# Buffers, preparation order and a state copy on GpSimd in a four-layer scan and window-attention kernel

## The chip, the cores and the metric

One core of one Trainium2 chip runs the whole program. The metric is device time in microseconds of one execution; the median of three executions is compared. Engines are named as in the profile: PE (TensorE matmul), PEld (its weight loads), DVE (VectorE), ACT (ScalarE), POOL (GpSimd) and SP (SyncE, which here only issues DMAs).

## The reference

The input x is (8, 56, 56, 192) in float32: eight images of 3136 pixels. Layer 0 splits the channels in two: the left 96 go through two 3x3 convolutions and a 1x1 one, the right 96 through a layer norm, a projection, a depthwise 3x3 convolution and a four-direction selective scan gated with a silu. Layers 1 and 2 are such scans alone, and layer 3 is a shifted-window attention (7x7 windows, six heads) with an MLP. The heart of layers 0 to 2 is the scan, over all 3136 pixels, in four orders k, for 192 channels d with 16 states n each:

```python
def step(h_prev, t):
    x_t, dt_t, B_t, C_t = t
    dA = jnp.exp(dt_t[..., None] * A)
    dBx = (dt_t * x_t)[..., None] * B_t[:, :, None, :]
    h = dA * h_prev + dBx
    y = jnp.einsum('bkdn,bkn->bkd', h, C_t)
    return (h, y)
```

Here dt is softplus of a small projection of x ("delta" below), and B and C are rows of another projection ("bc" below). Layer 3 in short:

```python
xw = jnp.roll(x, (-SS, -SS), axis=(1, 2))          # cut into 7x7 windows
attn = softmax(cos_sim(q, k) * scale + bias + mask)
x1 = shortcut + _ln(roll_back(attn @ v @ proj), norm1)
out = x1 + _ln(gelu(x1 @ fc1) @ fc2, norm2)
```

## The kernel before

**Scan steps.** `run` (L795) walks through 9216 steps: 8 images x 3 layers x 4 directions x 4 chunks of 784 pixels (a `Unit`) x 24 steps. A step has 128 partitions, 32 channels times 4 states, and 784 pixels. The 24 steps of a unit are two halves h of 12; a half is 96 channels, in 4 groups of states sg and 3 groups of channels j. One step s does, spread over five turns of the loop:

- `make` (L1037): ACT's exp of dsp (delta spread over the states) into a PSUM tile ps_x, of which there are two, and POOL's product db = usp x bt (du spread, and a B row broadcast), into one of four buffers;
- one turn later DVE's scan over ps_x and db. For three steps of four it writes ps_x, and DVE's product with ct gives hc. For each fourth (t % 4 == 3) the scan writes hc itself, and one turn later POOL multiplies hc by ct in place ("its own products");
- two turns after `make`, ACT copies the last column of the scan into `state` (L855), from which the same channels start in the next chunk, except after a last chunk;
- four turns later PE adds three hc into ps_y (`add_up`), and ACT merges ps_y into the layer's output.

Within a turn the order of issue is: state copy of s-2, exp and db of s, scan and product of s-1, POOL's product of s-2, `add_up`, `merge`, and then the pieces of other work. Every engine carries out its instructions in the order in which they are issued.

**Other work.** It is written as generators in three queues, and a yield of n puts the rest n turns off. `ahead` holds `prepare`, which makes delta and du for a half and spreads them with DMAs: two softplus pieces of 392 columns (matmul into a PSUM bank ps_p, relu into `delta`, abs, exp, ln and so on into `spe`, and POOL's add into `delta`), POOL's product `du`, then for each j the DMAs of `dsp` and `usp`, each with four buffers. `delta` and `du` have one buffer. `urgent` holds what follows a finished layer (`after`, and `project`, which writes the bc rows through the tile `bcx` to DRAM). `back` holds the next image's `ssm_front` and `conv_front` and the previous image's `attention_block`. At each turn pieces of `ahead` are issued freely, and those of the other two while a budget of charged PE and ACT time is left; SPARE and MOST (L1385) are its income and ceiling. `need` issues pieces at once, whatever turn it is, when a result is missing. All matmuls of other work share two PSUM banks; `all_banks` hands them out, the higher rank first.

**L3's rows.** `rows` (L1098) treats a row of eight windows: it loads a bias, the MLP's weights, runs `attention` and `mlp`, and `store` (L1354) transposes the result in four pieces, copies each to `ot` and stores it with DMAs on SP. The tag "wide" of pool q1 is one buffer that `qn`, `asq` and `hid` use in turn; `ot` shares the tag "pt" (two buffers of pool q2). After the last scan step, the last image's attention runs four rows at a time with six more banks (ps_t).

Of the kernel before, what the change touches and what calls it, by code (L numbers as in the profile page):

```python
# [31 lines left out]
F32 = mybir.dt.float32  # L32
# [4 lines left out]
HW = 56  # L37
L = HW * HW
C = 192
CH = 96  # L40
T = 448
ROWS = T // HW
NR = L // T
# [3 lines left out]
CK = 784  # L47
# [91 lines left out]
class Net:  # L139
    def __init__(self, ctx, tc, a, out):  # L140
        self.tc, self.nc, self.a, self.out = tc, tc.nc, a, out
        self.cp = ctx.enter_context(tc.tile_pool(name="const", bufs=1))
        self.dram = ctx.enter_context(tc.tile_pool(name="dram", bufs=1, space=bass.MemoryType.DRAM))
        self.dram2 = ctx.enter_context(
            tc.tile_pool(name="dram2", bufs=2, space=bass.MemoryType.DRAM)
        )
        ps = ctx.enter_context(tc.tile_pool(name="psp", bufs=1, space=bass.MemoryType.PSUM))
        self.banks = deque(ps.tile([128, 512], F32, name=f"ps_p{n}") for n in range(2))
        self.constants(ctx)
        self.wout = self.const("wout", [CH, 2, C])  # L150

        self.scans = ctx = ctx.enter_context(ExitStack())
        self.psum = ctx.enter_context(tc.tile_pool(name="psum", bufs=2, space=bass.MemoryType.PSUM))
        self.psum1 = ctx.enter_context(tc.tile_pool(name="psum1", bufs=1, space=bass.MemoryType.PSUM))
        big = ctx.enter_context(tc.tile_pool(name="big", bufs=1))
        self.bufs = [big.tile([CH, 2, L], F32, name=f"act{n}") for n in range(2)]
        for n in (1, 2, 3, 4, 5):
            setattr(self, f"s{n}", ctx.enter_context(tc.tile_pool(name=f"s{n}", bufs=n)))
        self.s6 = ctx.enter_context(tc.tile_pool(name="s6", bufs=HCS))
        self.ranks = self.s1.tile([CH, CK], F32, name="dts")  # L160
        self.aux = [self.s1.tile([CH, 2, HC], F32, name=f"aux{n}") for n in range(2)]
        self.nc.gpsimd.memset(self.ranks, 1.0)
        self.biasd = self.dram.tile([WT, 4, HEADS, WT], F32, name="biasd")
        self.done = set()
        self.nc = Engines(tc.nc)
        self.load = self.nc.load
        self.now, self.rank, self.asked = 0, 0, [-9] * 3
        self.ahead, self.urgent, self.back = deque(), deque(), deque()
        self.u0, self.sz, self.xl, self.u3, self.bcd = {}, {}, {}, {}, {}

# [195 lines left out]
            yield 2  # L366


    def bank(self, spare=0):


        (p,) = yield from self.all_banks(1, spare)
        return p

    def all_banks(self, n, spare=0):
        rank = self.rank
        while len(self.banks) < n + spare or any(at >= self.now - 1 for at in self.asked[rank + 1 :]):
            self.asked[rank] = self.now
            yield 1
        self.asked[rank] = -9  # L380
        return [self.banks.popleft() for _ in range(n)]
# [109 lines left out]
    def ssm_front(self, b):  # L491
# [3 lines left out]
        with tc.tile_pool(name="f1", bufs=1) as f1, tc.tile_pool(name="f2", bufs=2) as f2:  # L495
# [12 lines left out]
            grid = lambda p: p.rearrange("p (a b) -> p a b", a=ROWS)  # L508

            def depthwise(r, c, u):  # L510
                held = yield from self.bank(1)
                p = held[:CH, :T]
                for tap in range(9):
                    dy, dx = tap // 3, tap % 3
                    nc.tensor.matmul(
                        p, diag[:, c, tap, :], pads[r % 3][:, c, dy : dy + ROWS, dx : dx + HW],
                        start=tap == 0, stop=tap == 8,
                    )
                    if tap % 3 == 2:
                        yield 1  # L520
                yield 1
                nc.scalar.activation(u[:, c, :], p, AF.Identity, bias=self.v("conv2d_b", c))
                self.free(held)
                yield 1

            def gate(xnt, r, e, sz):
# [11 lines left out]
                self.free(held)  # L538
                yield 1

            for r in range(NR + 1):
                sz = u = None
                if r < NR:
                    tok = self.tokens(f2, b, r, "tokr", CH, C)
                    mv = f2.tile([TP, 4, 2], F32, name="mv")
                    rs = f2.tile([TP, 4], F32, name="rs0")
                    yield 2
                    for i in range(4):
                        st = f2.tile([TP, 6], F32, name="bnst")
                        nc.vector.bn_stats(st, tok[:, i, :])  # L550
                        nc.vector.bn_aggr(mv[:, i, :], st)
                        yield i % 2
                    nc.scalar.activation(rs, mv[:, :, 1], AF.Ln, bias=self.eps[:TP])
                    nc.scalar.activation(rs, rs, AF.Exp, scale=-0.5)
                    yield 1
                    for i in range(4):
                        nc.vector.tensor_scalar(
                            tok[:, i, :], tok[:, i, :], mv[:, i, 0:1], rs[:, i : i + 1],
                            ALU.subtract, ALU.mult,
                        )  # L560
                    yield 1
                    held = yield from self.bank()
                    p = held[:CH, :T]
                    for i in range(4):
                        nc.tensor.transpose(
                            p[:, i * TP : (i + 1) * TP], tok[:, i, :], self.ident[:TP, :TP]
                        )
                    yield LAG
                    xnt = f1.tile([CH, T], F32, name="xnt")
                    self.affine(xnt, p, self.v("ln_g"), self.v("ln_b"))  # L570
                    self.free(held)
                    yield 1
                    self.bottom(pads, r)
                    sz = f2.tile([CH, 2, T], F32, name="sz")
                    yield from self.together(2, [gate(xnt, r, e, sz) for e in range(4)])
# [13 lines left out]
    def conv_front(self, b):  # L589
# [3 lines left out]
        with tc.tile_pool(name="f1", bufs=1) as f1, tc.tile_pool(name="f2", bufs=2) as f2:  # L593
# [4 lines left out]
            grid = lambda p: p.rearrange("p (a b) -> p a b", a=ROWS)  # L598

            def conv(w, pads, r):  # L600
                held = yield from self.bank(1)
                p = held[:CH, :T]
                for tap in range(9):
                    dy, dx = tap // 3, tap % 3
# [7 lines left out]
                return p, held  # L612

            def first(r):
                tok = self.tokens(f2, b, r, "tokl", 0, CH)
                yield 2
                held = yield from self.bank()
                p = held[:CH, :T]
                for i in range(4):
# [21 lines left out]
            def third(r):  # L641
# [30 lines left out]
                yield from self.together(2, [last(c) for c in range(2)])  # L672
                nc.sync.dma_start(out=xld[:, :, r * T : (r + 1) * T], in_=xl)

            yield 2
            for r in range(NR + 2):
                if r < NR:
# [70 lines left out]
    def project(self, g, par, i):  # L748
# [7 lines left out]
        for q in range(2 * i, 2 * i + 2):  # L756
# [5 lines left out]
                    start=c == 0, stop=c == 1,  # L762
                )
            yield LAG
            t = self.s1.tile([128, HC], F32, name="bcx")[:W]
            nc.scalar.copy(t, p)
            self.free(held)
            yield 1
# [8 lines left out]
    def piece(self, queue, force=False):  # L777

        if not queue or (queue[0].at > self.now and not force) or queue[0].work.gi_running:
            return False  # L780
        task, rank = queue[0], self.rank
        self.rank = 2 if queue is self.ahead else int(queue is self.urgent)
        if not task.go(self.now):
            queue.remove(task)
        self.rank = rank
        return True
# [8 lines left out]
    def run(self):  # L795
# [25 lines left out]
        self.step = 0  # L821
        self.ahead.append(Task(self.prepare(units[0], 0, 0)))
        self.need(("half", 0))
        self.ahead.append(Task(self.prepare(units[0], 1, half)))
        for sg in range(NSG):
            self.load_bc(units[0], sg)
        made, weighed, copies = {}, {}, deque()
# [1 line left out]
        for s in range(S + 8):  # L829
            self.now += 1  # L830
            self.step = s
            for e in left:
                left[e] = min(left[e] + SPARE[e], MOST[e])

            t = s + half + 1
            if t < S and t % half == 0:
                self.ahead.append(Task(self.prepare(*steps[t][:2], t)))
            if s < S and s % half == 0:
                self.need(("half", s))
                U = steps[s][0]  # L840
                if s % (16 * NG) == 0:
                    if U.l == 0:
# [9 lines left out]
            if 0 <= t < S and not steps[t][0].last:  # L852
                U, h, sg, j = steps[t]
                end = CK - 1 if U.k < 2 else 0
                nc.scalar.copy(self.at_state(h, sg, j), made[t][:, end : end + 1])  # L855
            made.pop(t, None)
            if s < S:
                made[s] = self.make(*steps[s])
# [178 lines left out]
    def make(self, U, h, sg, j):  # L1037
# [3 lines left out]
        x = self.ps("x", 128, CK)  # L1041
        col = U.k * NG + (h * 3 + j) * NSG + sg
        self.nc.scalar.activation(x, d, AF.Exp, scale=self.A[U.l][:, col : col + 1])
        db = self.s4.tile([128, CK], F32, name="db")
        self.nc.gpsimd.tensor_mul(db, ub, self.B_[U, sg])
        return x, db

# [50 lines left out]
    def rows(self, b, wis, wqkv, wpr, f1b, q1, q2):  # L1098
# [18 lines left out]
        for n, wi in enumerate(wis):  # L1117
# [1 line left out]
            bias = q1.tile([WT, 2, HEADS, WT], F32, name="biasl")  # L1119
            kind = 2 * (wi == NW - 1)  # L1120
            nc.sync.dma_start(out=bias, in_=self.biasd[:, kind : kind + 2])
            yield 2
            wf1 = []
            for half in range(2):
                wf1.append(q2.tile([CH, 2, FF // 2], F32, name="wf1", tag="wf"))
# [3 lines left out]
            o = yield from self.mlp(x, f1b, wf1, q1, q2)  # L1129
            if n + 1 < len(wis):  # L1130
                x = yield from load(wis[n + 1])
            yield from self.store(o, wi, b, q2)

    def attention(self, x, wi, bias, wqkv, wpr, q1, q2):

# [215 lines left out]
        yield from self.block_norm(o, "n2", x, o, sq)  # L1351
        return o

    def store(self, o, wi, b, q2):  # L1354
        nc = self.nc

        def store(a):
            n = min(2, WS - a) * HW
# [4 lines left out]
                    p[:, CH * c : CH * c + CH], o[:, c, a * HW : a * HW + n], self.ident[:CH, :CH]  # L1363
                )
            yield LAG
            t = q2.tile([2 * HW, C], F32, name="ot", tag="pt")[:n]
            nc.scalar.copy(t, p)
            self.free(held)
            yield 1
# [12 lines left out]

ENDS = 4

SPARE = {"PE": 2.8, "ACT": 2.2, "DVE": 1.2, "POOL": 1.5}  # L1385
MOST = {"PE": 3.4, "ACT": 2.5, "DVE": 1.6, "POOL": 3.0}


def view(t, k, c, i, n):
# [124 lines left out]
```

## Time and profile before

| what | value |
| --- | --- |
| median of 3 runs | 31028.63 us (31018.46 to 31036.31) |
| the profiled execution | 31041.76 us, its span 31039.7 us |
| mean granted PE clock | 0.705 |
| first scan step starts, last one ends | 254.6 us, 30394.6 us |
| busy: DVE, POOL, PE, ACT | 25827.0, 24559.7, 19955.7, 17733.8 us |
| DMA queue of SP | 3455.30 MB, 48.4% of 16 engines' span |

In a group's line stand the line of the code (L109 is a helper through which most operations go, so groups are told apart by the tiles they write and read), engine, operation, output<-inputs, sizes and count; after the bar, busy time in us and the mean of one in ns; then the engine's idle time just before these instructions, and what ended it. In a line of waits stand who waited, for whom, the total in us, the number of times and the longest. In a line of the timeline stand start, duration, engine and operation, and in brackets the idle time before it and what ended that. An engine's idle time costs only where the end of the program hangs on it.

### The profile page before, as it was taken

To read this page: it belongs to the slowest core of one execution; us is meant where nothing else is said; L and a number is where in the kernel's file an instruction comes from. 1 tells how busy PE (TensorE), PEld (TensorE's weight loads), DVE (VectorE), ACT (ScalarE), POOL (GpSimd) and SP (SyncE) were. 2 spreads that over 40 slices of the span, in tenths; PEclk is the share of its full clock that TensorE was granted. 3 is DMA by queue.
4 is the path that set the end of the run, shared out by engine and by line. 5 is a ranking of instruction groups with operands and counts; after the bars stand their busy time and mean duration, and the time that the engine had idled before them with its cause. 6 is when DMAs were issued, how large, how long until landed. Compare 5 with 4: busy or idle time off the path is not lost. (4 is left out here: it accounts for less than half of the span.)

```text
span 31039.7 us, 270894 instructions
## 1 busy us (share of the span) xinstructions
PE 19955.7 (64%) x76788; PEld 6816.3 (22%) x76788; DVE 25827.0 (83%) x22213; ACT 17733.8 (57%) x35277; POOL 24559.7 (79%) x14751
## 2 busy tenths in 40 slices
PE   5665566666566666666666666666666666666657
PEld 1121112222122221222212222122221222222213
DVE  5888988888888888888888888888888888888882
ACT  4555555565556555566555655556655566555655
POOL 4888878888788788888788887878878888788782
PEclk7776667667676776777767767777676776777667
DMA  3554544445444455544554444544455444554451
GB/s 85 118 119 115 118 115 114 110 112 121 112 115 110 112 118 116 119 111 112 117 118 113 112 110 116 118 113 111 112 120 117 115 108 111 118 118 110 110 116 37
DMA packets 1538473, 3472.74 MB, mean 112 GB/s; under 512 B 345562, under 2 KB 538163, under 8 KB 1536964
## 3 DMA queue, kind: packets, MB, share of 16 engines
q1 hardware_dynamic: 1533700, 3455.30, 48.4%
q8 instruction: 607, 9.95, 0.1%
q14 instruction: 902, 7.39, 0.1%
q10 hardware_dynamic: 2496, 0.09, 0.0%
q0 software_dynamic: 768, 0.01, 0.0%
HBM read 1457.23 MB, written 147.89 MB: 52 GB/s over the span
## 5 line engine op out<-in xcount | busy, mean ns | idle before, releaser
L109 POOL TENSOR_TENSOR db<-usp,bt 128x784 f32<-128x784 f32 x9216 | 16895.6, 1854 | 1225.7 <-DMA usp<-du 937.9
L109 DVE TENSOR_TENSOR_SCAN ps_x<-ps_x,state,db 128x784 f32<-128x784 f32 x5184 | 9569.6, 1846 | 1504.5 <-ACT ps_x L109 955.2
L109 ACT ACTIVATE ps_x<-dsp,A 128x784 f32<-128x784 f32 x9216 | 8450.5, 917 | 2438.7 <-DVE hc L109 2260.6
L109 PE MATMUL ps_y<-hc,esum 128*32 128x392 f32 x36864 | 7539.7, 657 | 2143.1 <-POOL hc L109 1896.6
L109 DVE TENSOR_TENSOR hc<-ps_x,ct 128x784 f32<-128x784 f32 x6912 | 6736.3, 975 | 673.7 <-DVE ps_x L109 14.2
L109 POOL TENSOR_TENSOR hc<-hc,ct 128x784 f32<-128x784 f32 x2304 | 4247.2, 1843 | 3129.4 <-ACT state L109 2755.1
L109 DVE TENSOR_TENSOR_SCAN hc<-ps_x,state,db 128x784 f32<-128x784 f32 x1728 | 3179.1, 1840 | 563.5 <-ACT ps_x L109 216.6
L109 DVE TENSOR_TENSOR_SCAN ps_x<-ps_x,db 128x784 f32<-128x784 f32 x1728 | 3088.1, 1787 | 520.9 <-ACT ps_x L109 277.8
L109 ACT COPY state<-ps_x 128x1 f32<-128x1 f32 x5184 | 811.2, 156 | 4569.8 <-DVE hc L109 4560.1
L109 PEld LDWEIGHTS ps_y<-hc,esum 128*32 128x32 f32 x36864 | 1692.8, 131 | 7496.4 <-issue 3798.3
L109 PE MATMUL ps_p<-dts,dtw 13*96 13x392 f32 (+1 forms) x3072 | 1717.1, 658 | 1710.8 <-ACT state L109 369.9
L109 POOL TENSOR_TENSOR delta<-delta,spe 96x392 f32<-96x392 f32 x1536 | 1545.3, 1012 | 959.5 <-DVE spe L109 946.1
L109 PE MATMUL ps_y<-act,ident 96*96 96x392 f32 x2304 | 1655.1, 856 | 900.5 <-ACT act L109 828.3
L109 POOL TENSOR_TENSOR du<-delta,act 96x784 f32<-96x784 f32 x768 | 1569.8, 2044 | 0.2
L109 PE MATMUL ps_p<-act,wx 96*88 96x392 f32 (+1 forms) x1536 | 1024.7, 806 | 750.6 <-DVE spe L109 561.7
L109 ACT ACTIVATE delta<-ps_p 96x392 f32<-96x392 f32 x1536 | 741.0, 482 | 1210.9 <-DMA dsp<-delta 1114.9
L109 DVE TENSOR_TENSOR_SCAN hc<-ps_x,db 128x784 f32<-128x784 f32 x576 | 1025.4, 1780 | 266.5 <-ACT ps_x L109 107.3
L109 PEld LDWEIGHTS ps_p<-dts,dtw 13*96 13x96 f32 (+1 forms) x3072 | 473.8, 192 | 2879.0 <-ACT state L109 511.0
L109 PE MATMUL ps_p<-xip,diag 96*96 96x448 f32 x2016 | 893.4, 593 | 130.8 <-DVE spe L109 127.2
L109 ACT ACTIVATE ps_p<-ps_p 96x392 f32<-96x392 f32 x2076 | 931.2, 456 | 14.5 <-DVE ps_p L109 3.5
L109 ACT COPY act<-ps_y 96x784 f32<-96x784 f32 x768 | 927.1, 1207 | 8.5 <-PE ps_y L109 8.5
L109 ACT ACTIVATE ps_p<-spe,one 96x392 f32<-96x392 f32 x1536 | 902.0, 587 | 51.4
(212 smaller groups left out, 22537.6 us busy)
## 6 DMA issues: line engine op xcount, KB each, us to landing
dsp<-delta SPq DMA_DIRECT2D x2304, 392.0 KB
usp<-du SPq DMA_DIRECT2D x2304, 392.0 KB
bt<-bcd SPq DMA_DIRECT2D x1536, 392.0 KB
ct<-bcd SPq DMA_DIRECT2D x1536, 392.0 KB
wf<-in_wf SPq DMA_DIRECT2D x128, 288.0 KB
wf<-wf2d SPq DMA_DIRECT2D x128, 288.0 KB
bcd<-bcx SPq DMA_DIRECT2D x256, 134.8 KB
szd<-sz SPq DMA_DIRECT2D x56, 336.0 KB
```

Source lines behind the costliest of these rows:

```text
L109: return call(out, *args, **k)
```

## The change

- `prepare` for the next half is put into its queue after the turn's `need` of a half, twelve turns ahead, in place of thirteen.
- For t % 4 == 3 the state copy is issued on POOL in place of ACT, at the same place in the turn (ahead of that turn's db).
- `db` has three buffers in place of four, `bcx` two in place of one.
- `ot` is one tile of tag "wide" of pool q1, each store with its own columns of it; the pause of two turns after the bias load of a row is gone.
- `ssm_front` and `conv_front` load the tokens of band r + 1 when they begin band r, and their pause of two turns per band is gone.
- `all_banks`: the convolutions no longer ask for a spare bank; background work that isn't forced leaves one bank free at three turns of twelve.
- SPARE and MOST are 0.1 lower for PE and ACT.

```diff
+        self.now, self.rank, self.asked, self.forced = 0, 0, [-9] * 3, False
...
-    def all_banks(self, n, spare=0):
+    def all_banks(self, n):
         rank = self.rank
-        while len(self.banks) < n + spare or any(at >= self.now - 1 for at in self.asked[rank + 1 :]):
+
+        def kept():
+
+            return rank == 0 and not self.forced and (self.step + 1) % (NG // 2) < 3
+
+        while len(self.banks) < n + kept() or any(at >= self.now - 1 for at in self.asked[rank + 1 :]):
...
             def depthwise(r, c, u):
-                held = yield from self.bank(1)
+                held = yield from self.bank()
...
+            ahead = self.tokens(f2, b, 0, "tokr", CH, C)
+            yield 2
             for r in range(NR + 1):
                 sz = u = None
                 if r < NR:
-                    tok = self.tokens(f2, b, r, "tokr", CH, C)
+                    tok = ahead
+                    if r + 1 < NR:
+                        ahead = self.tokens(f2, b, r + 1, "tokr", CH, C)
                     mv = f2.tile([TP, 4, 2], F32, name="mv")
                     rs = f2.tile([TP, 4], F32, name="rs0")
-                    yield 2
...
             def conv(w, pads, r):
-                held = yield from self.bank(1)
+                held = yield from self.bank()
...
             def first(r):
-                tok = self.tokens(f2, b, r, "tokl", 0, CH)
-                yield 2
+                tok = toks.popleft()
+                if r + 1 < NR:
+                    toks.append(self.tokens(f2, b, r + 1, "tokl", 0, CH))
...
-            t = self.s1.tile([128, HC], F32, name="bcx")[:W]
+            t = self.s2.tile([128, HC], F32, name="bcx")[:W]
...
         task, rank = queue[0], self.rank
+        self.forced = force
...
         self.need(("half", 0))
-        self.ahead.append(Task(self.prepare(units[0], 1, half)))
...
-            t = s + half + 1
-            if t < S and t % half == 0:
-                self.ahead.append(Task(self.prepare(*steps[t][:2], t)))
             if s < S and s % half == 0:
                 self.need(("half", s))
+
+                t = s + half
+                if t < S:
+                    self.ahead.append(Task(self.prepare(*steps[t][:2], t)))
...
-                nc.scalar.copy(self.at_state(h, sg, j), made[t][:, end : end + 1])
+                copy = nc.gpsimd.tensor_copy if t % 4 == 3 else nc.scalar.copy
+                copy(self.at_state(h, sg, j), made[t][:, end : end + 1])
...
-        db = self.s4.tile([128, CK], F32, name="db")
+        db = self.s3.tile([128, CK], F32, name="db")
...
             nc.sync.dma_start(out=bias, in_=self.biasd[:, kind : kind + 2])
-            yield 2
...
-            yield from self.store(o, wi, b, q2)
+            yield from self.store(o, wi, b, q1)
...
-    def store(self, o, wi, b, q2):
+    def store(self, o, wi, b, q1):
         nc = self.nc
+        ts = q1.tile([128, 6 * BT + 16], F32, name="ot", tag="wide")
...
-            t = q2.tile([2 * HW, C], F32, name="ot", tag="pt")[:n]
+            t = ts[:n, a * C : (a + 1) * C]
...
-SPARE = {"PE": 2.8, "ACT": 2.2, "DVE": 1.2, "POOL": 1.5}
-MOST = {"PE": 3.4, "ACT": 2.5, "DVE": 1.6, "POOL": 3.0}
+SPARE = {"PE": 2.7, "ACT": 2.1, "DVE": 1.2, "POOL": 1.5}
+MOST = {"PE": 3.3, "ACT": 2.4, "DVE": 1.6, "POOL": 3.0}
```

More of the change, by code (lines that the diff above doesn't have):

```diff
@@ L166, in __init__ @@
         self.load = self.nc.load
-        self.now, self.rank, self.asked = 0, 0, [-9] * 3
+        self.now, self.rank, self.asked, self.forced = 0, 0, [-9] * 3, False
         self.ahead, self.urgent, self.back = deque(), deque(), deque()
@@ L366, in rel_bias, with bank @@
             yield 2
-    def bank(self, spare=0):
-        (p,) = yield from self.all_banks(1, spare)
+    def bank(self):
+        (p,) = yield from self.all_banks(1)
         return p
-    def all_banks(self, n, spare=0):
+    def all_banks(self, n):
         rank = self.rank
-        while len(self.banks) < n + spare or any(at >= self.now - 1 for at in self.asked[rank + 1 :]):
+        def kept():
+            return rank == 0 and not self.forced and (self.step + 1) % (NG // 2) < 3
+        while len(self.banks) < n + kept() or any(at >= self.now - 1 for at in self.asked[rank + 1 :]):
             self.asked[rank] = self.now
@@ L673, in third @@
                 nc.sync.dma_start(out=xld[:, :, r * T : (r + 1) * T], in_=xl)
+            toks = deque([self.tokens(f2, b, 0, "tokl", 0, CH)])
             yield 2
```

## The prediction

> **What bounds the kernel now.** I read the page's engine table first, then its groups, then the chain of waits by engine, then the timeline around one row of L3's stores.
>
> ```profile
> PE 19955.7 (64%) x76788; PEld 6816.3 (22%) x76788; DVE 25827.0 (83%) x22213; ACT 17733.8 (57%) x35277; POOL 24559.7 (79%) x14751
> ...
> L109 POOL TENSOR_TENSOR db<-usp,bt 128x784 f32<-128x784 f32 x9216 | 16895.6, 1854 | 1225.7 <-DMA usp<-du 937.9
> L109 DVE TENSOR_TENSOR_SCAN ps_x<-ps_x,state,db 128x784 f32<-128x784 f32 x5184 | 9569.6, 1846 | 1504.5 <-ACT ps_x L109 955.2
> ...
> L109 DVE TENSOR_TENSOR hc<-ps_x,ct 128x784 f32<-128x784 f32 x6912 | 6736.3, 975 | 673.7 <-DVE ps_x L109 14.2
> L109 POOL TENSOR_TENSOR hc<-hc,ct 128x784 f32<-128x784 f32 x2304 | 4247.2, 1843 | 3129.4 <-ACT state L109 2755.1
> ```
>
> DVE is fullest: 25827.0 of 31039.7 us, idle 5212.7. Four steps of the scan cost DVE 4 x 1.846 + 3 x 0.975 = 10.31 us and POOL 4 x 1.854 + 1.843 = 9.26 us, so POOL stands just behind DVE. Neither is full, so the price of an edit is what it adds to or takes from DVE's waits. Who ends them stands in the waits:
>
> ```profile
> DVE ps_x L109 <- ACT ps_x L109: 1233.0, 515, 14.1
> DVE ps_x L109 <- ACT state L109: 414.5, 152, 14.2
> DVE ps_x L109 <- POOL db L109: 337.0, 321, 7.7
> DVE hc L109 <- ACT ps_x L109: 323.9, 102, 10.2
> DVE bnst L109 <- DMA tokr<-in_x: 242.3, 24, 35.3
> ...
> DVE hc L109 <- ACT state L109: 163.8, 39, 25.0
> ```
>
> The four waits for ACT are scans that stand for a late exp: 1233.0 + 414.5 + 323.9 + 163.8 = 2135.2 us. POOL's db ends only 337.0 (and 79.8 for the form that writes hc). So: why is ACT late?
>
> ```profile
> ACT delta L109 <- DMA dsp<-delta: 1114.9, 386, 11.4
> ACT bcx L109 <- DMA bcd<-bcx: 759.1, 132, 16.4
> ACT ot L109 <- DMA out<-ot: 645.4, 124, 15.2
> ACT bcx L109 <- PE ps_p L109: 458.6, 191, 15.7
> ACT vt L109 <- PE ps_p L109: 361.1, 216, 4.3
> ACT hid L109 <- PE ps_p L109: 353.9, 243, 5.7
> ```
>
> ACT's queue is in order, so a copy that waits for a DMA holds the next exp. The first three are waits for a buffer that a DMA still reads. By the recorded starts I followed each scan that began over 0.25 us late on account of its exp back along ACT to ACT's longest wait in that step: 535 us of DVE's time lead to delta, 440 to bcx, 370 to ot, together 1345 of about 2170. The rest leads to PE waits and to table loads around the gelu.
>
> **The change part by part.**
>
> *Delta's preparation, one step later.* The relu into delta (one buffer) waits for the third dsp transfer of the half before: 386 waits, mean 2.89 us. Steps take (30394.6 - 254.6) / 9216 = 3.27 us. One step later, the mean wait is covered and the long ones (to 11.4) are cut. In the trace, where the relu already comes a step late (200 of 768 halves) it still waits 117 us in 65 cases. Scaled by 768/200 that leaves some 450 us of short ACT waits, mostly inside the 1.8 us that ACT has to spare (DVE needs 1.85 + 0.98 from the release of ps_x to the next scan, the exp 0.92 with its hand-over). I keep 105 of the 535: -430 (bounds -535 and, if preparation gets late for its half, +84, which is what POOL waits for usp at a half's first step now). The du product now lies six steps ahead of its half in 486 of 768 halves; five steps are 16 us, enough for a transfer.
>
> *bcx in two buffers.* The copy then waits for the transfer two back: 132 waits of mean 5.75 us get two more steps, 6.5 us. Of 440: -410 (bounds -440, -220).
>
> *ot as slices of one wide tile.* The four copies of a row no longer wait for each other's stores: of 370, -350 (bounds -370, -200). At the very end nothing comes of it: there SP issues a row's two stores every 1.75 us without a pause. But it adds a wait. The next row's first write into "wide" is qn's memset on POOL, and with the two idle steps after the bias load gone it comes in the step of the last store.
>
> ```profile
> 4983.64 0.31 ACT L109 COPY ot<-ps_p 56x192 f32<-56x192 f32 x1 [2.62 <-DMA out<-ot]
> ...
> 4986.14 1.96 SPq L1373 DMA_DIRECT2D out<-ot  x1
> ...
> 4988.15 1.21 SPq L1374 DMA_DIRECT2D out<-ot  x1
> ...
> 4989.52 0.11 POOL L109 MEMSET qn<- 96x16 f32 x1
> ```
>
> The last copy is at 4983.64, SP is through at 4989.36, and the copy at 4978.92 had its buffer 4.3 us after SP's issue of it ended (4974.62): landing is about 10 us after the copy. POOL would be there one step (3.3) after the copy and a product (1.84), and wait some 5 us; behind it in POOL's queue stand db products that DVE needs within two steps. Of 49 rows beside scans: bounds 0 and 49 x 8 = 390; I take 49 x 3.9 = +190. The Trainium skill (DMA: Bandwidth & Descriptors, "Anatomy of one DMA") puts the fixed part of a transfer at about 2 us, mostly the write's receipt; with that instead of the 4.3 us seen here the wait would be about 1.6 us a row, by estimate +80.
>
> *GpSimd copies the state of its own products.* Removed from ACT: 1728 copies of 0.189 us, 326 us, mostly where ACT waits for DVE anyway: 0. Removed from POOL: the product's wait for that copy, 2755.1 us in the row above; POOL's time, which DVE sees only through db. Added on POOL: 1728 copies of one column, between 0.10 us (its memset of 128x1) and 0.19 (ACT's copy): 170 to 330 us of POOL. What matters is the place: the copy stands ahead of db(s) and waits for scan(s-2), so every fourth step POOL loses its lead. From the end of that scan: copy 0.2, db 1.85, product 1.84, db 1.85, the last done at 5.74 plus hand-overs, while DVE (scan, product, scan, product, 0.1 us between) wants it at about 5.85. Nothing is spare, and what POOL does besides lands on DVE: per half of 12 steps two adds into delta (2 x 1.01) and du (2.04), 4.06 us; DVE's own softplus work in those steps (2 x 0.55 + 2 x 0.547 = 2.19) gives part back. Bounds: 0 (DVE still waits elsewhere and gives POOL time) and 768 x 1.87 = +1436. Nearest row: DVE's wait for db, 337.0 + 79.8 = 417 us with a lead of up to three steps; I take that it doubles, +420. A Trainium skill rule speaks against more POOL work: SBUF — State Buffer (what contends with what) says that DVE and GpSimd share a port pair by an exclusive lock, for DVE operations in a 2-port mode or with two SBUF inputs. The row that bears on it is the normalisation of tokr, 0.32 us with POOL idle and 1303 ns on the mean of 224. Were each copy to block DVE, the sum would grow by 1728 x 0.19 = 330; scans and products read one operand from PSUM, so I add nothing.
>
> *Bands of the fronts loaded ahead.* DVE's wait for tokr is 242.3; 171.3 of that lies before 420 us, where a band saves only its transfer (issue 90.20, landed 93.64: 3.4 us, some four bands before the first scan): -14, and -71 from the other 17. PE's wait for tokl (319.9) is not DVE's: 0.
>
> *db in three buffers:* POOL waits for DVE's release 124.9 + 38.3 us now, and the new copy waits later still: 0 (bounds 0, +163). *Banks kept at three steps of twelve, no spare one for convolutions:* ends of unknown sign, 0 (-100, +100). *SPARE down by 0.1:* ACT without exp and state copies is (17733.8 - 8450.5 - 811.2 - 326.2) / 9216 = 0.88 us a step against 2.1 allowed, so the limit is seldom the brake; 42 waited steps an image (two in each of 7 + 7 bands and 7 rows) fall away against it: 0. Bound: if the background fell 4% behind, the fronts' last xld store, now at 7.19 images, would pass its first reader at 7.28 and be forced: +570.
>
> Sum: -430 - 410 - 350 - 85 + 420 + 190 = -665 us. The profiled execution took 31041.8 us (span 31039.7), 13 above the median of 31028.6; from the median, 30364 us. A measurement of this kernel can tell about 0.2%, 62 us, from no change.
>
> **The rivals.**
>
> *POOL sets the pace (slower).* If the extra 4.06 us a half, less DVE's 2.19, lands in full, db costs 1436 in place of 420: -665 + 1016 = +351, 31380 us. It decides from 420 + 665 = 1085 us of added db wait, 1.4 us a half. For it: no spare time after the copy. Against it: DVE keeps some 3.9 ms of other idle, 5 us a half, in which POOL catches up. 0.17.
>
> *ACT's next wait steps in.* The same copies wait for PE too (458.6, 361.1, 353.9). If half of the gains (1275) come back so: -638 + 610 = -28, 31000 us. Against it: these waits are short (2.4, 1.7, 1.5 us) beside 1.8 to spare. 0.13, in equal parts same and faster.
>
> *The costs are covered.* POOL gets back what it waited for ACT, 2755.1, and the row wait hides: -1275 + 100, 29854 us. 0.20.
>
> The forecast has 0.50; its own range is 30100 to 30650.
>
> **How the numbers follow.** Low end 29850: about 0.08 lies under it, in the third rival. High end 31150: 0.12 of the first lies above. Faster by over 0.2%: 0.50 + 0.20 + 0.07 = 0.77; same 0.06; slower 0.17.
>
> **What would show it.** Right: ACT's waits delta, bcx and ot for DMAs fall from 2519 to under 700 us together, DVE's waits for ACT from 2135 to about 1000, DVE's wait for db rises to about 840, a row "POOL qn <- DMA out<-ot" of 200 to 400 us appears, "POOL hc <- ACT state" is gone, and DVE's share passes 84%. Wrong: a db wait over 1500, or DVE's waits for ACT still near 1700 under other names, or background work still open when an image ends.

## The result and the profile after

The changed kernel takes 31180.22 us (median of 5, 31160.79 to 31188.79), the kernel before in the same session 31028.63: a ratio of 1.0048, 95% interval 1.0033 to 1.0063. It is 0.5% slower, where 2.1% faster was forecast. The profiled execution took 31188.79 us, its span 31187.0.

The page's engine table and the groups that were shown of before:

```profile
PE 19669.7 (63%) x76788; PEld 6720.5 (22%) x76788; DVE 25799.5 (83%) x22213; ACT 17658.2 (57%) x33549; POOL 24785.2 (79%) x16479
...
L109 POOL TENSOR_TENSOR db<-usp,bt 128x784 f32<-128x784 f32 x9216 | 16950.0, 1855 | 1458.1 <-DMA usp<-du 981.9
L109 DVE TENSOR_TENSOR_SCAN ps_x<-ps_x,state,db 128x784 f32<-128x784 f32 x5184 | 9572.8, 1847 | 1719.9 <-POOL db L109 1266.5
...
L109 POOL TENSOR_TENSOR hc<-hc,ct 128x784 f32<-128x784 f32 x2304 | 4251.8, 1845 | 342.4 <-DVE hc L109 303.5
...
L109 POOL COPY state<-hc 128x1 f32<-128x1 f32 x1728 | 318.1, 184 | 2607.9 <-DVE hc L109 2592.1
```

None of the groups shown got dearer: db went from 1854 to 1855 ns, the scan from 1846 to 1847. DVE's idle time grew from 5212.7 to 5387.5 us, by 175, while the profiled span grew by 147, and what ends most of it before a scan is now POOL's db and no longer ACT's exp. The wait of POOL's own product (hc<-hc,ct) for ACT's copy, 2755.1 us, is gone, and nearly the same time, 2592.1 us, stands before POOL's new copy, one place earlier in its queue: ahead of a db. The chain of waits, DVE's part:

```profile
DVE ps_x L109 <- POOL db L109: 1864.3, 973, 35.2
DVE hc L109 <- PE ps_y L109: 476.0, 274, 6.9
DVE ps_x L109 <- ACT ps_x L109: 457.7, 214, 18.9
DVE hc L109 <- POOL db L109: 219.6, 61, 22.2
...
DVE hc L109 <- ACT state L109: 162.8, 27, 23.9
...
DVE hc L109 <- ACT ps_x L109: 95.1, 23, 6.4
...
DVE ps_x L109 <- ACT state L109: 67.1, 61, 4.5
```

DVE's wait for db went from 337.0 + 79.8 = 417 to 1864.3 + 219.6 = 2084 us, its wait for ACT from 2135 to 457.7 + 162.8 + 95.1 + 67.1 = 783. A count by the recorded times agrees. It takes each scan with over 0.25 us of idle time before it and asks which of its two operands ended last: with the exp as the last, 2169 us before and 772 after; with db as the last, 408 and 2088. Below, this is called late for exp and late for db. The three waits of ACT that the change aims at:

```profile
ACT delta L109 <- DMA dsp<-delta: 644.1, 303, 6.9
ACT ps_x L109 <- DMA dsp<-delta: 390.0, 129, 7.6
...
ACT bcx L109 <- DMA bcd<-bcx: 28.4, 13, 4.8
ACT qn L109 <- DMA out<-ot: 25.5, 4, 22.0
```

From 2519 us, delta, bcx and ot fell to 673 (ot's wait for its stores is out of the list), but a line that had 6.7 us before, the exp's own wait for dsp, stands at 390.0. New on POOL are these:

```profile
POOL state L109 <- DVE hc L109: 2592.1, 1264, 51.3
POOL db L109 <- DMA usp<-du: 981.9, 499, 6.2
POOL qn L109 <- DMA wf<-in_wf: 487.1, 35, 19.7
...
POOL qn L109 <- DMA out<-ot: 145.9, 10, 49.0
POOL qn L109 <- DMA bt<-bcd: 100.2, 5, 24.3
```

The memset of qn waits 849.1 us in all under several names (the transfer named is the last to land by the profile; what is waited for is the stores of ot, for with ot back in tag pt, in e2 below, 59 us are left). The timeline at the end of one of L3's rows shows what it is:

```profile
5619.87 0.31 ACT L109 COPY ot<-ps_p 56x192 f32<-56x192 f32 x1
...
5630.02 1.45 SPq L1384 DMA_DIRECT2D out<-ot  x1
...
5631.57 0.55 SPq L1026 DMA_DIRECT2D dsp<-delta  x1
...
5632.22 0.55 SPq L1026 DMA_DIRECT2D usp<-du  x1
5632.82 1.14 SPq L1383 DMA_DIRECT2D out<-ot  x1
5634.02 1.20 SPq L1384 DMA_DIRECT2D out<-ot  x1
...
5640.49 0.11 POOL L109 MEMSET qn<- 96x16 f32 x1 [14.79 <-DMA out<-ot]
...
5642.42 1.86 DVE L109 TENSOR_TENSOR_SCAN ps_x<-ps_x,state,db 128x784 f32<-128x784 f32 x1 [14.62 <-POOL db L109]
```

ACT made the last copy at 5619.87 without a wait, as intended. SP then needed until 5635.22 to issue the stores that the four copies had made ready (and five other transfers between them), the memset went at 5640.49, and here nearly all of POOL's 14.79 us arrived at DVE: 14.62.

### The profile page after: what moved, and what is told of

Its sections match the earlier page's. It is cut to its first block, busy times and chain, and to the rows that moved or that the text cites. A ratio compares the mean times of both kernels' runs of the same rounds, so it can differ in the third digit from the quotient of the medians.

```text
span 31187.0 us, 269851 instructions
## 1 busy us (share of the span) xinstructions
PE 19669.7 (63%) x76788; PEld 6720.5 (22%) x76788; DVE 25799.5 (83%) x22213; ACT 17658.2 (57%) x33549; POOL 24785.2 (79%) x16479
## 5 line engine op out<-in xcount | busy, mean ns | idle before, releaser
L109 POOL TENSOR_TENSOR db<-usp,bt 128x784 f32<-128x784 f32 x9216 | 16950.0, 1855 | 1458.1 <-DMA usp<-du 981.9
L109 POOL COPY state<-hc 128x1 f32<-128x1 f32 x1728 | 318.1, 184 | 2607.9 <-DVE hc L109 2592.1
L109 PE MATMUL ps_p<-xb,wf 96*128 96x392 f32 x1392 | 777.5, 713 | 506.9 <-DVE spe L109 280.8
```

What stands on the lines that cost most here:

```text
L109: return call(out, *args, **k)
```

## The experiments

Times are ratios to the kernel before, which ran beside each set (31029 us beside the change, 30993 to 31007 beside the others); a difference of 0.0010 is 31 us. The intervals are about 0.0015 to either side, so a difference of two runs under about 0.002 can't be told from none. The cuts of code show the lines that matter.

| run | ratio, 95% interval |
| --- | --- |
| the change | 1.0048 [1.0033, 1.0063] |
| e1_copy_on_act | 0.9922 [0.9907, 0.9937] |
| e2_ot_in_pt | 0.9975 [0.9964, 0.9985] |
| e3_copy_behind | 0.9907 [0.9890, 0.9923] |
| e4_both_undone ("the base") | 0.9846 [0.9831, 0.9861] |
| e5_spare | 0.9896 [0.9882, 0.9911] |
| e9_bcx_one | 0.9886 [0.9871, 0.9901] |
| e6_db_four_bcx_one | 0.9903 [0.9886, 0.9919] |
| e7_prepare_early | 0.9891 [0.9876, 0.9905] |
| f1_usp_first | 0.9809 [0.9794, 0.9823] |
| f2_ot_in_kn | 0.9826 [0.9810, 0.9843] |
| e8_banks | 0.9889 [0.9875, 0.9904] |
| f3_all | 0.9789 [0.9774, 0.9803] |
| g1_five | 0.9822 [0.9807, 0.9836] |
| g2_control | 0.9931 [0.9915, 0.9948] |
| g3_copy_only | 1.0072 [1.0057, 1.0087] |
| g4_best | 0.9787 [0.9772, 0.9801] |

**Which part makes it slow: the copy's place (A), qn's wait (B) or late background work (C).**

e1_copy_on_act undoes the copy:

```diff
-                copy = nc.gpsimd.tensor_copy if t % 4 == 3 else nc.scalar.copy
-                copy(self.at_state(h, sg, j), made[t][:, end : end + 1])
+                nc.scalar.copy(self.at_state(h, sg, j), made[t][:, end : end + 1])
```

> The changed kernel (31180 us) with one part undone: the state copy of every fourth step is ACT's again. Theory A (the copy stands ahead of the db product in GpSimd's queue and waits for the scan, so GpSimd loses its lead): the scans' waits for db fall from about 2090 to under 1300 us, the time to 30300-30500. Theory B (what costs is GpSimd's memset of qn, which waits for L3's stores): db waits stay near 1900, the time within 150 us of 31180. Theory C (background work that falls behind): no change, 31180.

e2_ot_in_pt undoes the place of ot:

```diff
-            t = ts[:n, a * C : (a + 1) * C]
+            t = q2.tile([2 * HW, C], F32, name="ot", tag="pt")[:n]
```

> The changed kernel with another part undone: ot has the two buffers of tag pt again. Theory B: the waits of qn for DMAs (about 840 us on GpSimd, of which some 710 reach the scans) go, ACT's waits for ot (645 us before, 370 of them at the scans) come back: 30800-30950 us. Theory A: qn's wait only takes the place of time that GpSimd would lose anyway, 31150-31400. Theory C: 31180 plus 370 for ACT, less what the scans gain.

e3_copy_behind leaves the copy on POOL and issues it behind the turn's db:

```diff
             if 0 <= t < S and t % 4 == 3:
                 U, h, sg, j = steps[t]
+                if not U.last:
+                    nc.gpsimd.tensor_copy(self.at_state(h, sg, j), kept[1])
                 nc.gpsimd.tensor_mul(weighed[t], weighed[t], self.C_[U, sg])
```

> The changed kernel with the state copy still on GpSimd, but issued behind the turn's db product, just ahead of GpSimd's own product, in place of ahead of db. Theory A (the place costs, not the work): as without the copy on GpSimd or a little better, 30250-30500 us, db waits under 1300. If the copy's own time (1728 x 0.184 = 318 us of GpSimd) is what costs: over 30900. Theory B: within 150 us of 31180.

e4_both_undone is e1 and e2 together.

> The changed kernel with both undone: copies on ACT, ot in tag pt. If the two costs are separate, the gains of the two single undoings add up (A and B together: 30000-30200 us). If one wait only uncovers the other, the sum is clearly less than the two. What remains of the change (delta one step later, bcx in two buffers, bands ahead) should then stand at 700 to 900 us below the kernel before.

Taking the copy off POOL gains 0.0126 (391 us), moving it behind db 0.0141 (437), undoing ot 0.0073 (226). With both undone it is 0.0202, and 0.0126 + 0.0073 = 0.0199: two separate costs, A and B, that add up. A is right on the place and wrong on the size: the gains of e1 and e3 are little over half of what it put to them (680 to 900 us). Scans late for db fall from 2088 to 1709 and 1693 us, where A had put under 1300. With ot undone as well it is 1095. Since the two gains add up, qn's wait does not hide a part of the copy's price: A had put too much to it. e3 says which property of the copy costs: its place. The same 1728 copies cost nothing that can be told behind db; the 0.0015 between e3 and e1 lies within the intervals. The base misses the 700 to 900 us put to it: it stands only 475 us below the kernel before, where the forecast had 925 for what is left of the change. The next runs take that apart.

**What is left of the change, part by part.** Theory D blames the third buffer that db lost, theory P the later preparation, theory C the budget. Each run is the base with one part as before (e7's line stands ahead of the turn's `need` again; e8 also gives the convolutions their spare bank back):

```diff
 e5_spare
-SPARE = {"PE": 2.7, "ACT": 2.1, "DVE": 1.2, "POOL": 1.5}
+SPARE = {"PE": 2.8, "ACT": 2.2, "DVE": 1.2, "POOL": 1.5}
 e9_bcx_one
-            t = self.s2.tile([128, HC], F32, name="bcx")[:W]
+            t = self.s1.tile([128, HC], F32, name="bcx")[:W]
 e6_db_four_bcx_one, besides
-        db = self.s3.tile([128, CK], F32, name="db")
+        db = self.s4.tile([128, CK], F32, name="db")
 e7_prepare_early
-                t = s + half
+            t = s + half + 1
 e8_banks
-        while len(self.banks) < n + kept() or ...
+        while len(self.banks) < n + spare or ...
```

> From here on the base is the run with copies on ACT and ot in tag pt (0.9846 of the kernel before, 475 us below it, where 925 were forecast for what is left of the change). This one also has the old budget (SPARE 2.8 and 2.2, MOST 3.4 and 2.5). Theory C (the lower budget lets background work fall behind: the next-to-last attention ran to the very end, the last image took 60 us more than the one before it): the background of image 7 ends at about 7.9 images, 50 to 120 us are gained. Theories D and P (below): within 40 us of the base.

The old budget is 0.0050 worse (155 us). The background does end earlier with it: the last store of the next-to-last attention comes at 7.67 images in place of the very end. Yet the six images between the first and the last take 3755 to 3761 us, in the base 3689 to 3754, and only the last is shorter (3633, against 3758). What C named does happen, and is repaid. No theory had expected a loss; that work which is spread thinner costs the scans less is a reading of these times, and no run isolates it.

> The base with one buffer of bcx again. If the forecast's term holds, ACT's wait for bcd<-bcx comes back (28 to about 750 us) and the time rises by 300 to 440 us. If the freed ACT time was no use, because the scans now wait for db instead, under 150 us.

The second buffer of bcx is worth 0.0040 (124 us), not 410, as the second reading had it: with it, scans late for exp fall from 1407 to 1202 us and those late for db rise from 954 to 1095. ACT's wait for bcd<-bcx falls from 524.8 to 36.6, while bcx's wait for PE rises from 613.5 to 726.1 and delta's for dsp from 766.3 to 890.6.

> The run with one bcx, and db in four buffers again (four of db and two of bcx don't fit together). Theory D (with three buffers GpSimd can't get far enough ahead, so its waits for usp, 1651 us, reach the scans, 666 us of them against 92 before): compared with the run that differs in db alone, 300 to 600 us less, scans' wait for db under 600. Theory P: within 60 us of it.

Four buffers of db are 0.0017 worse than three, within the intervals: no gain can be told. D falls.

> The base with the preparation put into its queue thirteen turns ahead again. Theory P (a turn later, usp lands too late for its half): scans' wait for db falls from about 1100 to under 700 us, while ACT's wait delta <- dsp costs less than that: 100 to 400 us gained. Theory D, and the forecast's first term: the relu's wait at the scans comes back, 300 to 450 us lost.

The later preparation is worth 0.0045 (140 us), not 430. P falls, for it had expected a gain from the earlier one. Here is where the rest went. The waits of POOL and ACT, first with the early preparation, then in the base:

```profile
POOL db L109 <- DMA usp<-du: 1006.4, 548, 6.7
...
ACT delta L109 <- DMA dsp<-delta: 1489.9, 496, 9.8
ACT ps_x L109 <- DMA dsp<-delta: 69.7, 49, 4.4
```

```profile
POOL db L109 <- DMA usp<-du: 1651.0, 792, 7.2
...
ACT delta L109 <- DMA dsp<-delta: 890.6, 355, 7.1
ACT ps_x L109 <- DMA dsp<-delta: 270.9, 94, 7.0
```

ACT's two lines lose 398 us together and POOL's gains 645. It is one transfer, or rather one pair: the relu waits until the third dsp of a half has landed, the exp of the third turn needs that dsp, and the db of the third turn needs the usp issued right behind it. Between a scan's end and the next, in us, by the turn within the half (means over all halves, from the recorded ends):

| run | 1st | 2nd | 3rd | 4th |
| --- | --- | --- | --- | --- |
| before | 2.39 | 3.75 | 3.30 | 3.60 |
| e7_prepare_early | 2.29 | 3.97 | 3.38 | 3.60 |
| the base | 2.55 | 3.17 | 3.85 | 3.31 |
| g2_control | 2.70 | 3.30 | 3.63 | 3.31 |
| g1_five | 2.63 | 3.21 | 3.18 | 3.31 |

With the preparation a turn later, the second turn gets 0.80 us back and the third loses 0.47 of it (the first loses 0.26, the fourth gains 0.29). The scans say what for: late for exp in the second turn falls from 624 to 119 us in all, late for db in the third rises from 143 to 553. That is theory T: one latency, waited for under another name. Its rivals: R, the transfer is as slow whatever stands ahead of it in SP's queue; G, POOL's pace, at 80% busy, takes whatever ACT gives.

> The base with the old rule for banks (a spare one for the convolutions, none kept). The forecast had 0 within 100 us. If the kept bank is what lets preparation start at once (relu eleven steps ahead in 738 halves of 768, where before it was late in 255), the old rule brings late halves back and costs 50 to 200 us.

The old rule for banks costs 0.0043 (133 us), as its second reading expected: du then comes five turns ahead of its half in 381 of 768 halves, in the base in 550.

**One latency, or POOL's pace.**

```diff
 f1_usp_first
-            for t, name in ((delta, "dsp"), (du, "usp")):
+            for t, name in ((delta, "dsp"), (du, "usp"))[:: -1 if j else 1]:
```

> The base (copies on ACT, ot in tag pt) with SP's order of two transfers turned round: for the second and third group of channels usp ahead of dsp. Theory T (taking away the relu's wait for the third dsp transfer only uncovers GpSimd's wait for the usp transfer issued right behind it, and that one hangs in SP's queue behind dsp, which waits for an exp): GpSimd's waits for usp fall from 1651 to under 900 us, 200 to 450 us are gained on the base. Rival R (the transfer itself takes the 7 us, whatever stands ahead of it): GpSimd's wait stays over 1400, the time within 60 us of the base; ACT might then wait for dsp, a loss.

POOL's wait for usp falls from 1651.0 to 628.9, the gain is 0.0037 (115 us), under what T expected. ACT tells why: its waits for dsp, in delta and ps_x, rise from 1161.5 to 1240.2 + 501.9 = 1742.1. In the third turn scans were late by 66 us for exp and 553 for db in the base; now it is 578 and 24. Whichever of the pair goes second is waited for. R, as stated, falls with POOL's wait. Yet where db has to wait for it, it starts 7.1 us after SP began to issue the third usp in the base and 6.0 here (medians): the place in the pair is 1.1 us of it, and what the rest is made of no run shows.

```diff
 f2_ot_in_kn, on e1 (each store takes the columns of its own number)
-        ts = q1.tile([128, 6 * BT + 16], F32, name="ot", tag="wide")
+        ts = q1.tile([128, 2 * BT], F32, name="ot", tag="kn")
```

> Copies on ACT, and ot as slices of one tile as in the change, but of the tag kn, whose next writer comes only after the next row's projections. Theory B (the slices are right, the tag is what makes GpSimd wait): ACT's waits for ot go (334 us at the scans in the base) and no qn wait comes: 200 to 340 us below the base, 430 to 570 below the run with the wide tag. If ACT's time is no longer what the scans wait for: under 100 below the base.

Against the tag "wide" (e1) this is 0.0096 better (298 us): the price of qn's wait. Against the base, where ACT waits 600 us for ot, it is only 0.0020 better (62 us), within the intervals. ACT's wait for ot, which led to 370 us of late scans in the trace of before, was worth next to nothing to the end. The scans show why: against the base, late for exp falls from 1202 to 868 us and late for db rises from 1095 to 1362; POOL's wait for usp, 1651.0 in the base, stands at 1799.7.

f3_all puts three things right: the copy behind db, ot in kn, usp first.

> The change with three things put right: the copy on GpSimd behind db, ot in tag kn, usp ahead of dsp. If the three costs are separate: the copy 40 us better than on ACT, ot 270 and usp 300 below the base, together 29900-30050 us. If they share one cause (GpSimd's lead), 30150-30300.

At 0.9789 it is the lowest so far, but 30347 us lies above both ranges. They had put 270 and 300 us to ot and usp; by their own runs the three parts gave 0.0015, 0.0020 and 0.0037, together 0.0072, and from the base to f3 it is 0.0057. That difference lies within the intervals, so whether the gains share a cause can't be told here. The last set gives the pair of transfers more time:

```diff
 g1_five (with one bcx, and six buffers of hc in place of seven, for the room)
-            while j and self.step < start - 4 + j:
+            while j and self.step < start - 5 + j:
-                s = self.s4.tile([128, CK], F32, name=name)
+                s = self.s5.tile([128, CK], F32, name=name)
```

> The base with five buffers of dsp and usp and the transfers of the second and third group of channels one turn earlier (for the room: one bcx, six hc). Theory T (one latency, from the issue of the third pair of transfers to its landing, is what relu, exp and db wait for in turn, at the third turn of each half): compared with the run that has the same room taken away, the third turn falls from 3.85 to about 3.3 us, GpSimd's wait for usp from about 1600 to under 700, 300 to 450 us gained. Theory G (GpSimd's pace, at 80% busy, takes what ACT gives): under 100 us gained, GpSimd's waits only change names.

> The base with one bcx and six hc, and nothing else: the measure for the run with five buffers. One bcx cost 124 us; one hc less may add to DVE's wait for PE's ps_y (474 us): 30600-30850 us by either theory.

The waits of POOL for usp, first in the control, then with five buffers:

```profile
POOL db L109 <- DMA usp<-du: 1458.6, 765, 7.9
```

```profile
POOL db L109 <- DMA usp<-du: 535.2, 276, 6.5
```

The pair differs in the buffers and the turn of issue alone, and in 0.0109: 338 us, inside T's 300 to 450. The third turn in the table falls by 0.45 us, which times 768 halves is 346: the whole gain lies there, for over the other eleven turns the differences cancel. Late for db in that turn falls from 411 to 102 us. T holds in the main, and G would have had under 100; of T's three waits the relu's falls too (739.5 to 233.0), but the exp's own does not (256.0 and 253.3). Six hc cost some 140 us (the control against e9_bcx_one), within what was put to the room; DVE's wait for PE's ps_y is 491.2 us in e9 and 1242.6 in the control.

g3_copy_only is the kernel before with the copy on POOL ahead of db and nothing else.

> The kernel before with one part of the change alone: the state copy of each fourth step on GpSimd, ahead of that turn's db. Forecast's term: +420 us (bounds 0 and +1436); undoing it in the changed kernel gave about 400. If the price is the lost lead and nothing else of the change, +300 to +450 here too. If it was so dear only because the change had made ACT faster, under +200.

The copy alone costs 0.0072 (223 us): between the two readings. In the changed kernel the same copy cost 391 to 437. Why it is dearer there is open: ACT holds DVE up less, but db also has three buffers in place of four, and no run has the copy with four in the changed kernel.

> The change put right: copy on GpSimd behind db, ot in tag kn, five buffers of dsp and usp a turn earlier, one bcx, six hc. Theory T: the best so far, 29950-30200 us. Theory G: about 30400, no better than with usp ahead of dsp.

g4_best (e3's copy, ot in kn, g1's buffers) reaches 0.9787, as f3_all does by another road. Both beat the kernel before by 2.1% and the changed one by 2.6%. At 30336 us it misses the 29950 to 30200 that T put to it, and lies nearer to G's 30400; "the best so far" can't be told from f3_all. From the base it gains 0.0059, which is what its parts gave one by one (0.0015, 0.0020, and 0.0024 for g1 with its room). So the size put to T was too large, while the place of its gain, the third turn, is shown by g1 and its control.

## Why the prediction failed

By the steps of its own sum, beside what the runs gave for that step alone:

| step | forecast, us | measured, us |
| --- | --- | --- |
| delta's preparation a turn later | -430 | -140 (e7 to base) |
| bcx in two buffers | -410 | -124 (e9 to base) |
| ot without waits on ACT | -350 | -62 (base to f2) |
| qn's wait for the stores | +190 | +298 (f2 to e1) |
| copy on POOL ahead of db | +420 | +391 (e1), +437 (e3); +223 in the kernel before (g3) |
| bands of the fronts ahead | -85 | not run by itself |
| banks kept | 0 | -133 (e8 to base) |
| SPARE lower | 0 | -155 (e5 to base) |
| db in three buffers | 0 | none that can be told (e6, e9) |

The right column is no sum: the four parts undone from the base (delta, bcx, banks, SPARE) come to 552 us, and the base as a whole is 475 below the kernel before.

**The step that failed is the pricing of the first three terms: a late scan traced back to ACT's wait was booked as gained nearly in full (1190 of 1345 us).** The tracing itself was right. It put 1345 us to delta, bcx and ot, and scans late for their exp fell by 1397 us. But a scan needs exp and db, and the stall was filled at the same time by whoever was next. Of the 1190 us, 326 came. For delta the runs name the next: POOL's wait for the usp of the same pair of transfers (e7, f1, g1). The forecast had that row before it (937.9 us for usp) and read it as an idle time of POOL, with 84 us of it as its bound. For bcx and ot the scans' own times name it as well, though no run takes it away:

| part | late for exp, us | late for db, us | together |
| --- | --- | --- | --- |
| delta (e7 to base) | 1794 to 1202 | 688 to 1095 | -185 |
| bcx (e9 to base) | 1407 to 1202 | 954 to 1095 | -64 |
| ot (base to f2) | 1202 to 868 | 1095 to 1362 | -67 |

Of 1131 us less for exp, 815 came back for db. POOL's wait for usp rises in each of the three: from 1006.4 and 1476.1 to 1651.0, and from there to 1799.7.

The copy's term was right in its reason: the place, not the work. POOL's copy takes 184 ns, near the upper end of its bounds, and that is not what costs, as e3 shows. That the size fits is in part luck: 420 was the guess that DVE's wait for db doubles, and in the kernel that the guess was read from the copy costs 223. The sign that was named as showing the forecast wrong, scans waiting over 1500 us for db, is what came (2084), but not from the copy alone, as the first rival had it: copy and qn together cost about 690 us, near the 610 that was put to them, and what turned the sum is that the gains did not come.

Qn's wait was seen and under-sized, 190 for 298. The step that erred is the landing "about 10 us after the copy". That was read where the four copies were spaced by their own waits. Without those, all are ready at once: over the 49 rows beside scans SP's last issue ends 14.0 us after the last copy (3.0 before), and the memset starts 19.7 us after it (medians). The 5.7 us from SP to the memset are near what was read; SP's own time was left out, though the prediction had it at 1.75 us for two stores, and a row has fourteen. POOL's memset waits 15.0 us on the mean in these rows, 735 in all, where some 5 us each was expected.

The fronts' bands were put at -85. The first scan starts at 237.9 us in place of 254.6, and DVE's wait for tokr fell from 242.3 to 13.8; but the next instruction on tokr, its normalisation, waits 121.7 us for ACT's rs in place of 11.5: half of it, again, under another name. What the scans got of it was not measured by itself.

The kept banks and the budget were put at 0 each and give 133 and 155 us. The budget's bound looked the wrong way: the background did fall behind, to the last image's end, which is also the third of the signs that were named, and the time still fell.

The second rival, half of the gains coming back under other names, was nearest the mark for the mechanism. It looked for them in ACT's waits for PE, where some are (bcx's wait for PE is 458.6 us before and 737.6 after), but most of the gain came back at POOL's db and the transfers it waits for.

## What to carry to other kernels

A stall that ends at engine X is worth at most the distance to the next thing that the same instruction needs: before a wait is booked as gained, look up when each of the instruction's other operands is ready, in the same turn, and take the smaller. In a queue that runs in order, an instruction that waits belongs behind the ones that others wait for; in the changed kernel the same copy cost 437 us ahead of one product and nothing that can be told behind it. A buffer's tag chooses who waits for its last reader: before sharing one, look which engine writes it next, how soon, and what stands behind that write.

## What the runs showed of the hardware

In the base the db of a half's third turn had to wait for its usp, a spread of 392 KB, in 378 of 768 halves (POOL idle over 0.3 us before it); there it started 6.6 to 8.7 us (5th to 95th percentile, median 7.1) after SP began to issue the transfer, though the issue itself takes 0.55 us in the median. With usp issued ahead of dsp (f1) the median is 6.0. One buffer and one turn more (g1 against g2) cut the halves with such a wait from 327 to 51. The 14 stores of a row in the changed kernel, seven of 40 KB and seven of 2 KB, take SP 13.3 us to issue, spread over 18.3 with other transfers between (medians of 49 rows). POOL's copy of one column takes 184 ns, ACT's 157 to 189. The DVE normalisation of tokr took 333 ns at most wherever POOL was idle throughout (105 of 224 before, 73 after); beside POOL's work its mean was 2169 ns before and 1460 after, so no lengthening by POOL's added copies can be seen.
